# A graph layer on one core: eight groups of x rows, B's rows per group, and a later subtraction and store

## The chip, the core and the metric

The kernel runs on one core of a Trainium2 chip. The metric is the device time of one execution in microseconds (us). The kernel before was run three times: 1989.7, 1991.37 and 1993.4 us, median 1991.37. A further execution was profiled, and the profile's numbers all come from that one.

## What is computed

One layer of a graph network over 12500 nodes (64 features each) and 200000 edges (32 features each, sorted by destination), then a residual and a layer norm. All data are float32.

```python
msg_in = jnp.concatenate([nodes[row], nodes[col], edge_features], axis=-1)
messages = relu(msg_in @ mW1 + mb1) @ mW2 + mb2
aggregated = jax.ops.segment_sum(messages, col, num_segments=nodes.shape[0])
upd_in = jnp.concatenate([nodes, aggregated], axis=-1)
x = layernorm(x + relu(upd_in @ uW1 + ub1) @ uW2 + ub2)
```

`row` is the source node of an edge (`src`), `col` its destination (`dst`). Sources are spread at random over the nodes; destinations rise from edge to edge.

## The kernel before

**Tables.** The first product of a message has three terms: source row times a part of mW1, destination row times another part (plus mb1), edge features times the last part. The first two depend on a node alone, so the kernel computes them once per node: table A (`tab_a`, 12500 rows of 128 numbers) and table B (`tab_b`). A is made at the head in 13 chunks of eight blocks of 128 nodes (`chunk_a`): the queue of ACT loads columns of x (`xl`), PE multiplies them (L381), ACT copies one half of the result and DVE the other (L391, L389) into a tile `tb`, and ACT's queue stores it to A (L395). There are two buffers for `xl`, two for `tb`, two for the PSUM result. Only the first chunk of B is made at the head, into B and into a small copy `B0` that the early edges read; the other chunks of B follow among the edge steps (`chunk_b`, L397).

**Edges.** The edges lie in 1563 tiles of 128. Eight tiles are a group (`SUB`, 196 of them), sixteen a super (`SUP`, 98). For each tile:

- POOL gathers 128 source rows by an indirect DMA, one per tile (`gather`, L147, L158). For the first `XG` = 7 groups it takes the raw rows of x (256 B each), which are transposed and multiplied by PE in the loop (`transpose`, and L257 in `node_part`), since A doesn't exist yet. From group 7 on it takes rows of A (512 B), which DVE adds (L263). The rows go into a pool of six buffers (`ROWB`); two groups of x rows share one, a group of A rows fills one. `frees` says after which group's use a buffer can be taken again.
- SP loads 32 consecutive rows of B that start at the tile's first destination, a window, into a tile `rhs` (`windows`, L216). One call of `windows(g)` loads the 16 windows of super g. The starts are read from `wint`, or for the first 20 supers from `win0`, a copy cut off at B0's end (L433).
- PE multiplies, per tile, a stack of 32 edge features and 32 rows of selection by the stack of mW1's part and the window (`edge_part`, L243). The selection is built on DVE per super from destinations that SP has loaded (`loadd` L173, `select` L185), and SP loads the edge features behind it (`load`, L204).
- DVE adds the gathered row, ACT applies Relu (`node_part`, L263 and L264), PE multiplies the result by a second selection so that each tile gives sums over its 32 nodes (`collect`, L276), and DVE adds them into a table of sums `comb` in SBUF (`aggregate`, L288). The second selection compares `drc` with the slot numbers; `drc` is destination minus window start, made by the subtraction in `relative` (L351) from two SP loads, in three parts: 128 columns at the head, and two more in steps 1 and 2.

**Updates.** When a stretch of up to 384 nodes has all its edges, an update turns sums into output: `columns`, `update`, `residual`, `norm`, one step apart, 54 times. The last of them, `norm`, scales on DVE into a tile `o` and then stores it from SP (L335).

**Order.** Each engine and each queue works in the order in which the program issues, which is written out by hand: first the head (the loop over chunks at L435, which also clears `comb` in eight strips, L441, and loads x columns into it, L344), then one step per group at L537 to L573. A step s issues, among others, `norm` of an update, the windows of the next super (in even steps), `node_part(s)`, `collect` and `aggregate` of group s-1, `select` and `load` of the next super (even steps), `loadd` (odd steps), a chunk of B, and `edge_part(s+1)`. Group numbers and step numbers are the same. The second half of the program (L576 on) is a general path that is skipped for these inputs.

Of the kernel before, what the change touches and what calls it, by code (L numbers as in the profile page):

```python
# [34 lines left out]
PADWIN = 1000000  # L35
EK, SK = 0, DE
ROWB = 6
XG = 7
NCH = 8
HB = NCH // 2  # L40
EARLY = NCH * P
GE = 20
# [22 lines left out]
def gnn_kernel(ctx: ExitStack, tc: tile.TileContext, x1T, x, eT, e_rows, src, dst, dst_row, wrow, wnext, whalf,  # L65
# [22 lines left out]
    nc = tc.nc  # L88
# [4 lines left out]
    A = dram.tile([NPAD, DH], F32, name="tab_a")  # L93
# [50 lines left out]
    def tiles(s):  # L144
        return range(s * SUB, min((s + 1) * SUB, NT))

    def gather(s):  # L147

        if s >= XG or s % 2 == 0:
            buf = rows.tile([P, SUB, DH], F32, name="xg")  # L150
        else:
            buf = xg[s - 1][0]
        d = DH if s >= XG else D
        a = buf.rearrange("p k (b d) -> p (k b) d", d=d)
        if s < XG:
            a = a[:, s % 2 * SUB:(s % 2 + 1) * SUB, :]
        for i, t in enumerate(tiles(s)):
            nc.gpsimd.indirect_dma_start(  # L158
                out=a[:, i, :], out_offset=None, in_=A[:, :] if s >= XG else x[:, :],
                in_offset=bass.IndirectOffsetOnAxis(ap=src_s[:, t:t + 1], axis=0))  # L160
        xg[s] = buf, a

    with tc.tile_pool(name="sup", bufs=2) as sup, tc.tile_pool(name="work", bufs=2) as work, tc.manual_schedule():
# [39 lines left out]
                q = 64 * b + EK  # L203
                nc.sync.dma_start(L[g][q:q + DE], eT[g, b])  # L204

        def windows(g):

            nt = min(SUP, NT - g * SUP)
            r = rhs[g % 2]
            w, tab, n = (win0, B0, EARLY - WIN + 1) if g < GE else (wint, B, N)  # L210
            _, ws = nc.values_load_multi_w_load_instructions(
                w[0:1, g * SUP:g * SUP + nt], engines=[ET.SP], min_val=0, max_val=n - 1,
                skip_runtime_bounds_check_because="destinations are node numbers")
            for i in range(nt):
                q = SK + 64 * (i % 2)
                nc.sync.dma_start(r[q:q + WIN, i // 2, :], tab[bass.ds(ws[i], WIN), :])  # L216

        def transpose(s):

# [8 lines left out]
        def parts(n):  # L228

            if n == SUB:  # L230
                return [(slice(None), slice(None))]
            return [(slice(b, b + 1), slice((n - b + 1) // 2)) for b in range(2) if n > b]

        def edge_part(s):

# [11 lines left out]
        def node_part(s):  # L247

            n = len(tiles(s))
            pc = pcs.pop(s)  # L250
            h = work.tile([P, 2, SUB // 2, DH], F32, name="h")
            if s < XG:
                xt = xs.pop(s)
                for i in range(n):
                    k, b = divmod(i, 2)
                    q = 64 * b
                    nc.tensor.matmul(pc[:, b, k, :], xt[q:q + 64, k, :], w1a[q:q + 64], start=False,  # L257
                                     stop=i + 2 >= n)
                nc.scalar.activation(h, pc, AF.Relu)
            else:  # L260
                a = xg.pop(s)[1].rearrange("p (k b) f -> p b k f", b=2)
                for b, m in parts(n):
                    nc.vector.tensor_tensor(h[:, b, m], pc[:, b, m], a[:, b, m], op=ALU.add)  # L263
                    nc.scalar.activation(h[:, b, m], h[:, b, m], AF.Relu)  # L264
            hs[s] = h

        def collect(s):
# [57 lines left out]
            us[u] = (n0, py, mv, sd)  # L325

        def norm(u):
            n0, py, mv, sd = us.pop(u)
# [17 lines left out]
        def relative(a, b):  # L346

            wbc = work.tile([P, WCH], I32, name="wbc", tag="tb")
            nc.sync.dma_start(dst_s[:, a:b], dst[:, a:b])
            nc.sync.dma_start(wbc[:, :b - a], wrow[:, a:b].broadcast_to([P, b - a]))  # L350
            nc.vector.tensor_tensor(drc[:, a:b], dst_s[:, a:b], wbc[:, :b - a], op=ALU.subtract)  # L351
# [77 lines left out]
        for r in rhs:  # L429
            for o in (EK, EK + 64):  # L430
                nc.sync.dma_start(r[o:o + DE], mW1[2 * D:, :].unsqueeze(1).broadcast_to([DE, SUP // 2, DH]))
        relative(0, 8 * SUP)
        nc.vector.tensor_scalar(win0, wint[:, :GE * SUP], float(EARLY - WIN), None, op0=ALU.min)  # L433
        Q = NCOL // 4
        for k, c in enumerate(range(0, NB, NCH)):  # L435
            chunk_a(c)
            if k == 0:
                chunk_b(0, [B0v, Bv])
                windows(0)
            if k < 8:  # L440
                nc.vector.memset(comb[:P if k < 4 else ONE, k // 4, k % 4 * Q:(k % 4 + 1) * Q], 0.0)  # L441
# [95 lines left out]
        for s in range(last + 3):  # L537
            g, j = divmod(s, SUP // SUB)
            while gathered < NSUB and frees(gathered) < s:
                gather(gathered)  # L540
                gathered += 1
            if s - 2 in due:
                norm(due[s - 2])
            if j == 0 and g + 1 < NSUP:
                windows(g + 1)
            if s < NSUB:
                node_part(s)
            if s in due and s < last:
# [24 lines left out]
            rest(s)  # L573


    flag = nc.values_load(flag_i[0:1, 0:1], min_val=0, max_val=2 * EBULK,  # L576
# [163 lines left out]
```

## Time and profile before

| what | us |
|---|---|
| median of the three runs | 1991.37 |
| the profiled execution | 1995.25 |
| its span, first to last instruction | 1993.5 |
| PE busy, 7851 matmuls | 1364.8 (68%) |
| DVE busy | 908.7 (46%) |
| ACT busy | 348.4 (17%) |
| POOL busy, 1572 instructions | 1477.0 (74%) |
| DMA, mean over the span | 106 GB/s |
| TensorE clock granted, mean | 0.559 |

A profile row names a source line, an engine, an operation and the tiles it writes and reads; times are microseconds from the span's start. "Idle before" is the time for which the engine did nothing ahead of an instruction, and the name behind the arrow is what ended that wait, as far as semaphores tell. "issue" means that it waited for nothing that the profile shows. SPq and ACTq are the queues on which SP and ACT issue DMAs; the time in such a row is that of issuing, and the transfer lands later.

### The profile page before, as it was taken

What the parts mean: (1) busy time and instruction counts of PE and PEld (TensorE: products, weight loads), DVE (VectorE), ACT (ScalarE), POOL (GpSimd) and SP (SyncE); (2) the same over time, 40 slices, a digit from 0 to 9 for tenths busy, and PEclk for the clock granted to TensorE, in tenths of its full rate; (3) what the DMA queues carried; (4) which work ended last, traced back from release to release, by engine and by line L of the source; (5) the groups of instructions that cost most, each with busy time, mean ns of one, the idle gap of its engine ahead of it and who ended that gap; (6) DMA issues with size and microseconds to landing.
All of it is one profiled execution on the core that took longest, in us unless ns stands there. A gap on an engine that the chain in (4) does not pass through costs nothing.

```text
span 1993.5 us, 31593 instructions
## 1 busy us (share of the span) xinstructions
PE 1364.8 (68%) x7851; PEld 1211.9 (61%) x7851; DVE 908.7 (46%) x2661; ACT 348.4 (17%) x479; POOL 1477.0 (74%) x1572
## 2 busy tenths in 40 slices
PE   3678876656566666566667766676686776776867
PEld 3577875556555666556566665665575655665756
DVE  5347544434343444444444444444454545454544
ACT  1121111111111111111111111121212121212111
POOL 7577777777777777777777777777777777777773
PEclk7665555555555555555555555556555656565555
DMA  8745554433333333333333333334333333333331
GB/s 219 217 118 151 158 139 117 115 88 100 88 99 89 99 91 99 91 97 92 99 91 94 97 100 91 97 96 102 95 99 97 96 100 98 98 98 98 98 98 39
DMA packets 244401, 211.74 MB, mean 106 GB/s; under 512 B 80542, under 2 KB 209022, under 8 KB 243824
## 3 DMA queue, kind: packets, MB, share of 16 engines
q0 software_dynamic: 50016, 100.70, 20.4%
q1 hardware_dynamic: 178644, 98.69, 17.9%
q10 hardware_dynamic: 15554, 10.31, 1.8%
q8 instruction: 63, 1.03, 0.2%
q14 instruction: 124, 1.02, 0.2%
HBM read 190.78 MB, written 18.68 MB: 105 GB/s over the span
## 4 chain that ended last, share of the span: by engine, by line
POOL 53%; issue 25%; PE 9%; DMA 8%; DVE 3%; SPq 1%; ACT 1%; DVEq 0%; ACTq 0%; POOLq 0%
POOL xg L158 53%; DMA xg<-tab_a,src_s 5%; PE ph L276 3%; DMA xl<-in_x1T 2%; PE pc L243 2%; DVE comb L288 2%; PE pu L304 1%; PE py L315 1%; DVE h L263 1%; PE pb L381 1%; PE pu L305 1%; PE py L316 1%; DMA l<-in_eT 0%; PE ph L274 0%; DVE o L333 0%
## 5 line engine op out<-in xcount | busy, mean ns | idle before, releaser
L158 POOL DMA_INDIRECT xg<-tab_a,src_s x1507 | 1423.0, 944 | 470.0 <-issue 444.2
L276 PEld LDWEIGHTS ph<-sel,h 128*128 128x128 f32 x3126 | 610.2, 299 | 34.4 <-issue 34.4
L276 PE MATMUL ph<-sel,h 128*128 128x32 f32 x3126 | 601.0, 363 | 0.0
L263 DVE TENSOR_TENSOR h<-pc,xg 128x1024 f32<-128x1024 f32 (+1 forms) x190 | 230.8, 1215 | 770.4 <-DMA xg<-tab_a,src_s 720.7
L243 PE MATMUL pc<-rhs,l 64*128 64x128 f32 x3126 | 408.9, 415 | 62.8 <-DMA l<-in_eT 24.5
L288 DVE TENSOR_TENSOR comb<-comb,ph 128x64 f32 x1563 | 345.6, 221 | 202.1 <-ACT xw L297 83.0
L243 PEld LDWEIGHTS pc<-rhs,l 64*128 64x128 f32 x3126 | 352.7, 303 | 82.8 <-DVE rs L330 30.3
L264 ACT ACTIVATE h<-h 128x1024 f32<-128x1024 f32 (+1 forms) x190 | 199.2, 1049 | 915.0 <-DVE h L263 881.7
L304 PE MATMUL pu<-comb,w2u 128*128 x108 | 88.9, 927 | 255.9 <-DVE comb L288 255.9
L274 PE MATMUL ph<-selb,one 128*128 128x256 bf16 x196 | 75.4, 384 | 239.7 <-DVE comb L288 156.8
L274 PEld LDWEIGHTS <-one 128*128 128x128 bf16 x196 | 27.3, 139 | 272.2 <-DVE comb L288 252.8
L304 PEld LDWEIGHTS pu<-comb,w2u 128*128 128x128 f32 x108 | 27.1, 312 | 271.3 <-DVE comb L288 271.3
L185 DVE TENSOR_TENSOR l<-l,cps 128x1024 f32<-128x1024 int32 (+1 forms) x101 | 123.3, 1221 | 4.8 <-DMA l<-in_dst_row 1.3
L197 ACT CAST selb<-sel 128x512 bf16<-128x512 f32 x98 | 60.4, 616 | 329.3 <-DVE sel L189 308.7
L315 PE MATMUL py<-ux,xw 128*128 128x64 f32 x324 | 87.0, 362 | 0.7 <-ACT hTu L307 0.7
L316 PE MATMUL py<-u,hTu 128*128 128x64 f32 x324 | 84.3, 354 | 0.0
L305 PE MATMUL pu<-xw,uz 128*128 128x384 f32 x108 | 80.1, 846 | 0.0
L307 ACT ACTIVATE hTu<-pu,ub_s 128x384 f32<-128x384 f32 x54 | 31.3, 580 | 270.7 <-PE pu L305 270.7
L315 PEld LDWEIGHTS py<-ux,xw 128*128 128x128 f32 x324 | 68.9, 263 | 10.8 <-issue 6.3
L316 PEld LDWEIGHTS py<-u,hTu 128*128 128x128 f32 x324 | 70.3, 268 | 0.0
L189 DVE TENSOR_TENSOR sel<-cps,drc 128x512 f32<-128x512 f32 x98 | 66.8, 682 | 0.1
L158 POOL DMA_INDIRECT xg<-in_x,src_s x56 | 53.0, 946 | 18.4 <-issue 16.5
(73 smaller groups left out, 420.2 us busy)
## 6 DMA issues: line engine op xcount, KB each, us to landing
l<-in_dst_row SPq DMA_DIRECT2D x196, 128.0 KB
l<-in_eT SPq DMA_DIRECT2D x196, 128.0 KB
rhs<-tab_b SPq DMA_DIRECT2D x1563, 16.0 KB
xg<-tab_a,src_s POOLq DMA_INDIRECT x1507
tab_b<-tb SPq DMA_DIRECT2D x13, 512.0 KB
tab_a<-tb ACTq DMA_DIRECT2D x12, 512.0 KB
out<-o SPq DMA_DIRECT2D x54, 96.0 KB
comb<-in_x1T SPq DMA_DIRECT2D x6, 520.0 KB
```

What stands on the lines that cost most here:

```text
L158: nc.gpsimd.indirect_dma_start(out=a[:, i, :], out_offset=None, in_=A[:, :] if s >= XG else x[:, :], in_offset=bass.IndirectOffsetOnAxis(a ...
L185: nc.vector.tensor_tensor(l[r], l[r].bitcast(I32), node[r].unsqueeze(2).broadcast_to([r.stop - r.start, SUP // 2, P]), op=ALU.is_equal)
L243: nc.tensor.matmul(pc[:, b, k, :], L[g][q:q + 64, m, :], rhs[g % 2][q:q + 64, m, :], start=s >= XG or k == 0, stop=s >= XG)
L263: nc.vector.tensor_tensor(h[:, b, m], pc[:, b, m], a[:, b, m], op=ALU.add)
L264: nc.scalar.activation(h[:, b, m], h[:, b, m], AF.Relu)
L274: nc.tensor.matmul(ph[:, :n, 1, :], one0, SB[g][:, k0:k0 + n, :], start=True, stop=True)
L276: nc.tensor.matmul(ph[:, i, 0, :], h[:, i % 2, i // 2, :], S[g][:, k0 + i, :], start=True, stop=True)
L288: nc.vector.tensor_tensor(to, to, ph[:, i], op=ALU.add)
L304: nc.tensor.matmul(pu, w2u, comb[:, 0, bass.ds(n0, UB * P)], start=True, stop=False)
L305: nc.tensor.matmul(pu, uz, xw, start=False, stop=True)
L315: nc.tensor.matmul(py[:, i], xw[:, i * P:(i + 1) * P], ux, start=True, stop=False)
L316: nc.tensor.matmul(py[:, i], hT[:, i * P:(i + 1) * P], u2, start=False, stop=True)
```

## The change

Six edits go together.

- `XG` is 8: group 7 also takes rows of x and goes through transpose and matmul. The first gather from A is that of group 8, the 65th.
- `windows` takes a group in place of a super and loads its eight windows; step s issues `windows(s + 2)`, in each step. The head issues `windows(0)` and `windows(1)`.
- In the head, the subtraction of the first 128 columns (`relative`, with its two loads) moves from ahead of chunk one into chunk five (k == 4), and `win0` with the first windows from ahead of, and out of, chunk one into chunk three (k == 2).
- `norm` no longer stores; a new `store` issues the DMA at the end of the same step.
- A gathered group of A rows lies in its buffer in the order in which the PSUM tile holds it (even tiles, then odd ones), so the add reads and writes plain slices; `parts` returns slices for that.
- `columns` of the last update stands right behind `aggregate` in step 196.

```diff
-XG = 7
+XG = 8
...
-        d = DH if s >= XG else D
-        a = buf.rearrange("p k (b d) -> p (k b) d", d=d)
         if s < XG:
-            a = a[:, s % 2 * SUB:(s % 2 + 1) * SUB, :]
+            a = buf.rearrange("p k (b d) -> p (k b) d", d=D)[:, s % 2 * SUB:(s % 2 + 1) * SUB, :]
+        else:
+            a = buf.rearrange("p (b k) d -> p k b d", b=2)
...
-        def windows(g):
-            nt = min(SUP, NT - g * SUP)
+        def windows(s):
+            g = s // (SUP // SUB)
+            o = s % (SUP // SUB) * SUB
+            nt = len(tiles(s))
...
-                nc.sync.dma_start(r[q:q + WIN, i // 2, :], tab[bass.ds(ws[i], WIN), :])
+                nc.sync.dma_start(r[q:q + WIN, (o + i) // 2, :], tab[bass.ds(ws[i], WIN), :])
...
-                a = xg.pop(s)[1].rearrange("p (k b) f -> p b k f", b=2)
-                for b, m in parts(n):
-                    nc.vector.tensor_tensor(h[:, b, m], pc[:, b, m], a[:, b, m], op=ALU.add)
-                    nc.scalar.activation(h[:, b, m], h[:, b, m], AF.Relu)
+                hf, pf = (t.rearrange("p b k f -> p (b k) f") for t in (h, pc))
+                a = xg.pop(s)[0]
+                for m in parts(n):
+                    nc.vector.tensor_tensor(hf[:, m], pf[:, m], a[:, m], op=ALU.add)
+                    nc.scalar.activation(hf[:, m], hf[:, m], AF.Relu)
...
+            us[u] = (n0, o)
+
+        def store(u):
+            n0, o = us.pop(u)
             nc.sync.dma_start(out[bass.ds(n0, UB * P), :].rearrange("(c p) d -> p c d", p=P), o)
...
-        relative(0, 8 * SUP)
-        nc.vector.tensor_scalar(win0, wint[:, :GE * SUP], float(EARLY - WIN), None, op0=ALU.min)
...
             if k == 0:
                 chunk_b(0, [B0v, Bv])
+            if k == 2:
+                nc.vector.tensor_scalar(win0, wint[:, :GE * SUP], float(EARLY - WIN), None, op0=ALU.min)
                 windows(0)
+                windows(1)
+            if k == 4:
+                relative(0, 8 * SUP)
...
-            if j == 0 and g + 1 < NSUP:
-                windows(g + 1)
+            if s + 2 < NSUB:
+                windows(s + 2)
...
             if 1 <= s <= NSUB:
                 collect(s - 1)
                 aggregate(s - 1)
+            if s == NSUB:
+                columns(K - 1)
...
-            if s == NSUB:
-                columns(K - 1)
...
             rest(s)
+            if s - 2 in due:
+                store(due[s - 2])
```

More of the change, by code (lines that the diff above doesn't have):

```diff
@@ L152, in gather @@
             buf = xg[s - 1][0]
-        d = DH if s >= XG else D
-        a = buf.rearrange("p k (b d) -> p (k b) d", d=d)
         if s < XG:
-            a = a[:, s % 2 * SUB:(s % 2 + 1) * SUB, :]
+            a = buf.rearrange("p k (b d) -> p (k b) d", d=D)[:, s % 2 * SUB:(s % 2 + 1) * SUB, :]
+        else:
+            a = buf.rearrange("p (b k) d -> p k b d", b=2)
         for i, t in enumerate(tiles(s)):
             nc.gpsimd.indirect_dma_start(
-                out=a[:, i, :], out_offset=None, in_=A[:, :] if s >= XG else x[:, :],
+                out=a[:, i, :] if s < XG else a[:, i // 2, i % 2, :], out_offset=None, in_=A[:, :] if s >= XG else x[:, :],
                 in_offset=bass.IndirectOffsetOnAxis(ap=src_s[:, t:t + 1], axis=0))
@@ L211, in windows @@
             _, ws = nc.values_load_multi_w_load_instructions(
-                w[0:1, g * SUP:g * SUP + nt], engines=[ET.SP], min_val=0, max_val=n - 1,
+                w[0:1, s * SUB:s * SUB + nt], engines=[ET.SP], min_val=0, max_val=n - 1,
                 skip_runtime_bounds_check_because="destinations are node numbers")
@@ L230, in parts @@
             if n == SUB:
-                return [(slice(None), slice(None))]
-            return [(slice(b, b + 1), slice((n - b + 1) // 2)) for b in range(2) if n > b]
+                return [slice(0, SUB)]
+            return [slice(b * SUB // 2, b * SUB // 2 + (n - b + 1) // 2) for b in range(2) if n > b]
         def edge_part(s):
@@ L327, in norm @@
         def norm(u):
-            n0, py, mv, sd = us.pop(u)
+            n0, py, mv, sd = us[u]
             rs = work.tile([P, UB], F32, name="rs")
```

## The prediction

> **What bounds the kernel now.** I read the page's chain of work that ended last, then the waits of POOL, then POOL's timeline at both ends of its work, then DVE and SP between 0 and 80 us. The chain names the engine:
>
> ```profile
> POOL 53%; issue 25%; PE 9%; DMA 8%; DVE 3%; SPq 1%; ACT 1%; DVEq 0%; ACTq 0%; POOLq 0%
> ```
>
> POOL's gathers (L158) and the "issue" time between them make 78% of the span. POOL's waits (line, what it waited for: us in total, times, longest) and its timeline (start us, us, ..., idle before) show the one hole:
>
> ```profile
> POOL xg L158 <- issue: 460.7, 1511, 0.3
> POOL xg L158 <- DMA rhs<-tab_b: 10.9, 1, 10.9
> ```
>
> ```profile
> 72.20 0.94 POOL L158 DMA_INDIRECT xg<-in_x,src_s  x1 [0.30 <-issue]
> 84.04 0.94 POOL L158 DMA_INDIRECT xg<-tab_a,src_s  x1 [10.90 <-DMA rhs<-tab_b]
> ...
> 1965.22 0.95 POOL L158 DMA_INDIRECT xg<-tab_a,src_s  x1 [0.30 <-issue]
> ```
>
> A gather takes 0.944 us, the next starts 0.30 later: one per 1.249 us (the timeline's median). 1563 gathers, first at 2.88, last at 1965.22: 1562 x 1.249 = 1950.9 of 1962.3 us. Of the 11.4 left over, 10.6 is one wait, before the 57th gather, the first to read tab_a. The table is being written until then (its last store is issued at 78.93 on ACT), so I read the "rhs<-tab_b" in that row as a mislabel of tab_a's landing. After it POOL never waits again. Behind POOL the tail is 1993.5 - 1966.2 = 27.3 us. So the span is: start 2.9 + gathers at POOL's pace + 10.6 hole + 0.8 other + tail 27.3. PE, DVE and ACT follow the gathers (DVE's adds at L263 waited 720.7 us for them).
>
> **What the skill says.** "DMA: Bandwidth & Descriptors", section "SWDGE vs HWDGE vs iDMA": a GpSimd core runs code to compute the descriptors of a gather. The trace agrees: 128 rows cost 0.944 us of POOL from tab_a (512 B rows) and 0.946 from x (256 B rows), so the source of a group changes nothing in POOL's work. Same page, "Issuing engines are not separate DMA queues": transfers of SP, ACT and GpSimd run on the same 16 DMA engines. The trace agrees: the DMA share is 0.89 to 0.93 between 20 and 84 us, and ACT's loads of x columns slow down when SP's comb loads begin. Same page, "Anatomy of one DMA": the wait for a semaphore is on the issuing sequencer, so what is behind it on SP stands. The trace agrees: SP's waits hold 493 us before L204, for select. "SBUF — State Buffer", section "Who interferes with whom": a VectorE instruction with two SBUF inputs contends with a GpSimd instruction that reads SBUF. Two gathers agree: they took 1.71 and 1.26 us beside L351's subtractions (0.77 + 0.32 lost); L263, which has one input in PSUM, delays none.
>
> **The change, part by part.**
>
> *Eight groups of x rows.* Gathers 57 to 64 now read x and need no table. POOL goes on at 72.20 + 1.25 = 73.45 and fills the hole with 8 x 1.249 = 9.99 us of work; gather 65, now the first on tab_a, is ready to issue at 83.45. The number of gathers stays 1563. If tab_a is complete by 83.4, the hole is gone: -10.6. If the table lands as before (gather at 84.04), 0.6 is left: -10.0. The added work lies on PE and ACT: group 7 takes 4 transposes (1.1 us, L224), a copy (0.59, L225) and 16 matmuls (1.9 to 2.1, L257) in place of an add of 1.21 on DVE, about +2 to 3 us on the consumers' path, under POOL. The gathers of 73 to 83 us bring 8 x 128 x 256 B = 0.26 MB beside tab_a's last stores, about 1 us of DMA at the 240 GB/s of that stretch.
>
> *Subtraction in chunk five, win0 and the windows in chunk three.* Before, DVE stood 17.57 us at the head for the subtraction's operand:
>
> ```profile
> 19.68 0.29 DVE L351 TENSOR_TENSOR drc<-drc,wbc 128x128 f32<-128x128 int32 x1 [17.57 <-DMA wbc<-in_wrow]
> ...
> 20.29 0.67 DVE L389 COPY tb<-pb 128x512 f32<-128x512 f32 x1
> ...
> 22.71 2.75 DVE L441 MEMSET comb<- 128x3232 f32 x1 [0.62 <-issue]
> ```
>
> PE's products of chunk one are ready at about 12, so its copy can come 8 us earlier. From there a chunk costs DVE 0.62 (copy) + 0.62 (before the memset) + 2.75 = about 4 us: copies at 12.3, 19 (it waits for its tb buffer, the store of chunk one), 23.3, 27.8, 31.8. Before they were at 20.3, 25.4, 29.3, 33.2, 37.2: some 5 us gained at chunk five. Then it is partly given back: the subtraction now waits, in chunk five, for wbc, which SP issues behind win0 (about 24) and 16 window loads. These took 26.93 to 38.59 before, 0.5 to 0.73 each, so 8 to 11.7 us; with two issues more wbc goes out at 33 to 37 and lands 4.5 later (15.11 to 19.6 before): 37.5 to 41.5. DVE stands until then and clears one more strip of comb; the sixth copy comes at 41 to 44.5 (before: 41.06). SP's comb loads (before from 39.94 on, 3.4 MB) start at 35 to 39 and have the DMA engines nearly to themselves while DVE stands. What remains then is bound by bytes: before, 41 to 83.7. I estimate that tab_a is complete 7 us earlier to 3 us later than before, 77 to 87, most likely 80.5. That is ahead of 83.45, and the hole is closed. Cost taken: 0. A DVE subtraction beside a gather, by the 0.32 and 0.77 above for 411 and 1024 columns: up to 0.3 for 128 columns. Taken: 0.3.
>
> *Are the buffers free in time?* With the hole gone POOL reaches group g 10.6 us sooner, and its row buffer comes free only when the add of group g-6 is done. From L263's ends and the starts of the groups' first gathers before:
>
> ```profile
> 142.32 1.22 DVE L263 TENSOR_TENSOR h<-pc,xg 128x1024 f32<-128x1024 f32 x1 [1.71 <-PE pc L243]
> ...
> 173.80 1.23 DVE L263 TENSOR_TENSOR h<-pc,xg 128x1024 f32<-128x1024 f32 x1 [0.28 <-DMA xg<-tab_a,src_s]
> ```
>
> The add of group 8 ended at 143.5, that of group 11 at 175.0; POOL will want their buffers at 155.03 - 10.6 = 144.4 and 185.01 - 10.6 = 174.4. Had the consumers not moved, with the 2 us of added work they would be 1 to 3 us late. They begin when PE has done the last chunk, 78.25 before, and move forward with the table: at 3 us earlier the stall is nothing, at 0 it is about 2.6. After 250 us the lead is 45 us and more (278.56 to 324.88 for group 25). Taken: 0; kept for the range: up to 3.
>
> *Windows per group.* Same 1563 loads, 8 per step instead of 16 per two steps, each still two steps (20 us) ahead of its matmul. No load of B's rows is named among PE's waits before, so nothing is removed from the path. The windows of an odd group now stand on SP behind load (L204), which waits for select. Eight loads take 4.4 us (8.74 for 16 at 776.72), landing about 3: some 12 us of lead remain. Cost 0, under cover of the lead; if that is gone, PE and then POOL pay.
>
> *Store at the step's end.* SP waited 112.1 us in 52 times before L335 for DVE's o, with loads behind it, but no consumer was late for it. The store goes out a few us later; o has two buffers and 37 us between updates. 0. In the last step nothing stands behind it: 0 in the tail.
>
> *Gather layout and parts.* The add reads the same 1024 elements in another order; 1.215 us is bounded by 1.1 and 1.35 and lies under POOL. Last group: still two adds and two Relus. columns(K-1) moved within step 196, where no load, chunk or edge part is issued between the two places: 0.
>
> Sum: -10.6 + 0.3 = -10.3. The profiled execution took 1995.25, its span is 1993.5, with 1.75 around it; it becomes 1983.2 and 1984.95. It stood 3.9 above the median of the runs shown. On the median: 1991.4 - 10.3 = **1981.1**.
>
> **Rivals.** (1) The table is late: the deferred subtraction holds DVE, the last chunks slip, and the new first table gather finds a hole of 3 to 7 us (table at 86 to 90). For it: wbc behind 16 loads on SP, and one tb buffer given to wbc, so chunk six copies only when chunk five's store has landed. Against it: bytes, not DVE, bound 41 to 84 (DMA share 0.89 and more). Gives about 1986. (2) The consumers catch POOL at groups 14 to 17: 3 us, about 1984. (3) The hole closes but the end doesn't move: 1989 to 1991; against it, POOL works without a gap to 1965.22, and the tail hangs on its last groups. (4) Slower: SP's order. An odd group's windows wait behind load, hence for DVE's select; if SP fell behind by over its 12 us of lead, PE's edge part would start late in each of 98 supers, and POOL stop for buffers. Price: 1 us per super is 98 us. It decides once the 45 us of row-buffer lead are used too; to end 0.2% above the median the supers must lose 10.3 + 4 us beyond both leads. SP issues some 6 us in a 10 us step, which speaks against it. About 2010.
>
> **Numbers.** Forecast (1981.1, own range 1978 to 1984): 0.67. Rival 1: 0.15. Rival 2: 0.09. Rival 3: 0.05. Rival 4: 0.04. Within 0.2% (4 us, about what a measurement of this kernel can tell from no change) lies rival 3 alone: faster 0.91, same 0.05, slower 0.04. The range holds forecast and rivals 1 and 2 but for their tails: 1977.5 to 1987.
>
> **What would show it.** POOL without an idle time over 1 us between 2.9 and its last gather, which starts near 1954.9; 64 gathers from x; the subtraction (128 columns) between 37 and 42 with DVE idle before it; comb loads on SP from 35 to 39; steps from 72 to 77 on; a tail of 27 us. It is wrong if POOL shows a new wait near 83 us (rival 1) or for DVE between 120 and 185 (rival 2), if PE's edge parts wait for rhs (rival 4), or if POOL ends 10 us earlier and the span doesn't (rival 3).

## The result and the profile after

| | before | after |
|---|---|---|
| median of six runs, us | 1990.53 | 1997.91 |
| lowest and highest | 1988.38 to 1993.4 | 1994.82 to 2000.5 |
| the profiled execution | 1995.25 | 2000.5 |
| its span | 1993.5 | 1998.4 |
| end of POOL's last gather | 1966.17 | 1971.22 |
| from there to the end | 27.3 | 27.2 |

The ratio of after to before is 1.0034, 95% interval 1.0021 to 1.0047: the change made the kernel slower by about 7 us. It was predicted to be 10 us faster. The profiled spans differ by 4.9, and POOL's last gather ends 5.05 later, so what happened is to be read on POOL.

The chain that ended last, by engine, in the kernel after:

```profile
POOL 48%; issue 21%; DMA 15%; PE 11%; DVE 4%; ACT 1%; SPq 0%; DVEq 0%; ACTq 0%; POOLq 0%
```

POOL and its issue time are still the larger part, but DMA and PE have gained shares: the chain now leaves POOL in places. POOL's waits in the kernel after (line, what it waited for: us in total, times, longest) and its timeline (start, us, ..., idle before) say where:

```profile
POOL xg L158 <- issue: 440.4, 1444, 0.6
...
POOL xg L158 <- DVE h L266: 10.6, 2, 6.1
POOL xg L158 <- DMA rhs<-tab_b: 5.2, 1, 5.2
```

```profile
82.67 0.94 POOL L158 DMA_INDIRECT xg<-in_x,src_s  x1 [0.30 <-DMA tab_a<-tb]
88.83 0.94 POOL L158 DMA_INDIRECT xg<-tab_a,src_s  x1 [5.21 <-DMA rhs<-tab_b]
...
153.61 0.94 POOL L158 DMA_INDIRECT xg<-tab_a,src_s  x1 [4.58 <-DVE h L266]
...
189.63 0.94 POOL L158 DMA_INDIRECT xg<-tab_a,src_s  x1 [6.07 <-DVE h L266]
...
1970.27 0.94 POOL L158 DMA_INDIRECT xg<-tab_a,src_s  x1 [0.30 <-issue]
```

The one hole of 10.6 us has become three. Less the usual 0.30, they are 4.9 at the first gather from the table (now the 65th), 4.3 at the first gather of group 14 and 5.8 at that of group 17: 15.0 in place of 10.6. Smaller waits make 1.4 in place of 0.5. Together that is 5.3 more, which is the 5.05 but for 0.2. The gathers themselves go at 1.249 us as before.

**The first hole** comes from DVE. DVE's timeline in chunk five of the kernel after, and SP's ahead of it:

```profile
36.19 0.63 DVE L396 COPY tb<-pb 128x512 f32<-128x512 f32 x1
...
47.84 0.29 DVE L358 TENSOR_TENSOR drc<-drc,wbc 128x128 f32<-128x128 int32 x1 [11.03 <-DMA wbc<-in_wrow]
48.75 2.75 DVE L451 MEMSET comb<- 63x3232 f32 x1 [0.61 <-DVE drc L358]
51.42 0.62 DVE L396 COPY tb<-pb 128x512 f32<-128x512 f32 x1
```

```profile
29.05 12.03 SPq L218 DMA_DIRECT2D rhs<-tab_b  x16
41.12 0.42 SPq L356 DMA_DIRECT2D drc<-in_dst  x1
42.09 0.37 SPq L357 DMA_DIRECT2D wbc<-in_wrow  x1
42.51 0.88 SPq L204 DMA_DIRECT2D l<-in_eT  x2
43.43 27.11 SPq L351 DMA_DIRECT2D comb<-in_x1T  x7
```

The operand's load stands behind 16 window loads and leaves at 42.09; DVE waits 11.03 us for it and copies no chunk from 36.8 to 51.4. (The subtraction's operand also takes one of the two `tb` buffers, but the sixth copy follows the memset without an idle time, so no buffer held it.) The sixth chunk's copy is 10.4 us later than before (41.06), and the last store of the table is issued at 83.98 (before: 78.93). So 5 of the 10 us that the eighth group filled come back.

**The other two holes** come from the consumers, the engines that use the gathered rows and so free the row buffers. DVE's wait for the second part of the subtraction, before:

```profile
96.20 1.23 DVE L351 TENSOR_TENSOR drc<-drc,wbc 128x1024 f32<-128x1024 int32 x1 [5.68 <-DMA wbc<-in_wrow]
```

DVE in the kernel after, between 100 and 190 us:

```profile
101.90 1.22 DVE L358 TENSOR_TENSOR drc<-drc,wbc 128x1024 f32<-128x1024 int32 x1 [7.03 <-DMA rhs<-tab_b]
...
152.12 1.23 DVE L266 TENSOR_TENSOR h<-pc,xg 128x1024 f32<-128x1024 f32 x1 [0.28 <-issue]
...
182.01 1.76 DVE L505 TENSOR_REDUCE mm<-drc 128x1 f32<-128x1563 f32 x1
183.70 1.76 DVE L506 TENSOR_REDUCE mm<-drc 128x1 f32<-128x1562 f32 x1
...
188.13 1.23 DVE L266 TENSOR_TENSOR h<-pc,xg 128x1024 f32<-128x1024 f32 x1 [0.28 <-issue]
```

Group 8's add ends at 153.35 and group 14's first gather, which takes that buffer, starts at 153.61; group 11's add ends at 189.36 and group 17's gather starts at 189.63. Before, the adds ended at 143.5 and 175.0, and POOL came for the buffers at 155.03 and 185.01. The consumers are 10 and 14 us later than then; their lead of 10 to 11.5 us is used up. Ahead of these adds stand two things that the change did not touch: the second part of the subtraction (DVE waited 5.7 for its operand before, 7.03 now) and the work of step 10: small products of the update's weights and, with two reductions over `drc`, a check of the input (some 8 us on DVE in all).

### The profile page after: what moved, and what is told of

It reads as the page before. It is cut to its first block, busy times and chain, and to the rows that moved or that the text cites. A ratio compares the mean times of both kernels' runs of the same rounds, so it can differ in the third digit from the quotient of the medians.

```text
span 1998.4 us, 31764 instructions
## 1 busy us (share of the span) xinstructions
PE 1355.4 (68%) x7871; PEld 1202.9 (60%) x7871; DVE 907.4 (45%) x2660; ACT 348.7 (17%) x480; POOL 1477.0 (74%) x1572
## 3 DMA queue, kind: packets, MB, share of 16 engines
q14 instruction: 125, 1.02, 0.2%
## 4 chain that ended last, share of the span: by engine, by line
POOL 48%; issue 21%; DMA 15%; PE 11%; DVE 4%; ACT 1%; SPq 0%; DVEq 0%; ACTq 0%; POOLq 0%
POOL xg L158 48%; DMA xg<-tab_a,src_s 11%; PE ph L279 4%; PE pc L245 2%; DVE comb L291 2%; DMA tab_a<-tb 2%; PE pb L388 1%; PE pu L307 1%; PE pc L259 1%; PE py L318 1%; PE pu L308 1%; DVE h L266 1%; PE py L319 1%; PE ph L277 0%; DMA comb<-in_x1T 0%
## 5 line engine op out<-in xcount | busy, mean ns | idle before, releaser
L279 PEld LDWEIGHTS ph<-sel,h 128*128 128x128 f32 x3126 | 603.2, 295 | 33.9 <-issue 33.8
L279 PE MATMUL ph<-sel,h 128*128 128x32 f32 x3126 | 594.1, 360 | 0.0
L266 DVE TENSOR_TENSOR h<-pc,xg 128x1024 f32<-128x1024 f32 x189 | 229.5, 1215 | 769.2 <-DMA xg<-tab_a,src_s 735.1
L245 PEld LDWEIGHTS pc<-rhs,l 64*128 64x128 f32 x3126 | 351.5, 301 | 80.8 <-DVE rs L333 27.2
L267 ACT ACTIVATE h<-h 128x1024 f32<-128x1024 f32 x189 | 198.2, 1049 | 915.4 <-DVE h L266 823.8
L277 PEld LDWEIGHTS <-one 128*128 128x128 bf16 x196 | 27.1, 138 | 279.7 <-DVE comb L291 259.5
L307 PEld LDWEIGHTS pu<-comb,w2u 128*128 128x128 f32 x108 | 27.1, 311 | 265.2 <-DVE comb L291 265.2
L158 POOL DMA_INDIRECT xg<-in_x,src_s x64 | 60.6, 948 | 21.3 <-issue 18.3
```

What stands on the lines that cost most here:

```text
L158: nc.gpsimd.indirect_dma_start(out=a[:, i, :] if s < XG else a[:, i // 2, i % 2, :], out_offset=None, in_=A[:, :] if s >= XG else x[:, :], ...
L245: nc.tensor.matmul(pc[:, b, k, :], L[g][q:q + 64, m, :], rhs[g % 2][q:q + 64, m, :], start=s >= XG or k == 0, stop=s >= XG)
L266: nc.vector.tensor_tensor(hf[:, m], pf[:, m], a[:, m], op=ALU.add)
L267: nc.scalar.activation(hf[:, m], hf[:, m], AF.Relu)
L277: nc.tensor.matmul(ph[:, :n, 1, :], one0, SB[g][:, k0:k0 + n, :], start=True, stop=True)
L279: nc.tensor.matmul(ph[:, i, 0, :], h[:, i % 2, i // 2, :], S[g][:, k0 + i, :], start=True, stop=True)
```

## Experiments

The theory after the result: (a) the eighth group is right and closes the hole, if the table is in time; (b) the table is late since DVE waits in chunk five for a load that was queued last; (c) the holes at groups 14 and 17 are a consequence of POOL's earlier arrival, meeting old stalls of DVE (second subtraction, step 10) and the longer step of group 7. The rivals: the eighth group itself costs more than it gives (against a); the table is bound by bytes, and DVE's wait is covered (against b); the windows' or the store's new order delays the consumers (against c).

"Holes" below are the idle times of POOL less the usual 0.30, in the order: first gather from the table; group 13; group 14 (its first two gathers together); group 17. Each profile is of one execution. Medians stand beside those of the kernel before on the same chip; the ratio, with its 95% interval, rests on all the times and can differ a little from the ratio of the medians.

### First six runs: two chips on which POOL is not the bound

Four single edits were run together, two of them again on another chip. The first and its repeat, against the kernel before:

```diff
-XG = 7
+XG = 8
```

> The kernel before with one edit, eight groups of x rows. Theory (three stalls: the table is late because DVE waits for the deferred subtraction; group 7 as an x step holds the consumers; the checks on DVE in step 10 hold them again): the table is ready near 84 as before, the hole shrinks from 10.6 to about 0.6, but the eighth x step costs the consumers some 5 us, so POOL waits about 4 us before group 14 and 2 before group 17; POOL's excess over its pace is about 7 against 11.4, time about 1986.5 (4 below before). Rival (the new order of SP's queue makes the later stalls): no stall at groups 14 and 17 here, time about 1980.5.

> The kernel before with one edit, eight groups of x rows; a repeat on another chip, since on the first one the kernel before itself took 2808 us[...]. Theory (three stalls: the table is late because DVE waits for the deferred subtraction; group 7 as an x step holds the consumers; the checks on DVE in step 10 hold them again): the table is ready near 84 as before, the hole shrinks from 10.6 to about 0.6, but the eighth x step costs the consumers some 5 us, so POOL waits about 4 us before group 14 and 2 before group 17; POOL's excess over its pace is about 7 against 11.4, time about 1986.5 (4 below before). Rival (the new order of SP's queue makes the later stalls): no stall at groups 14 and 17 here, time about 1980.5.

The second and its repeat, against the kernel after: both loads of the first subtraction stay in the head, into a tile of their own, and only the subtraction is in chunk five.

```diff
+        w0 = first_loads(8 * SUP)
         Q = NCOL // 4
...
             if k == 4:
-                relative(0, 8 * SUP)
+                nc.vector.tensor_tensor(drc[:, :8 * SUP], dst_s[:, :8 * SUP], w0, op=ALU.subtract)
```

> The changed kernel, with the two loads of the deferred subtraction issued in the head ahead of the chunks, into a tile of their own; the subtraction stays in chunk five. Theory (DVE's wait for these loads delays the table): DVE doesn't wait in chunk five, the table is ready before 83.4, no hole before the 65th gather; consumers start at 78 or sooner; stalls at groups 14 and 17 stay in part (6 to 9 us in sum): 1986 to 1990. Rival (the table is bound by bytes, the comb loads beside it, whatever DVE does): hole of 2 to 5 us stays, time 1993 to 1998.

> The changed kernel, with the two loads of the deferred subtraction issued in the head ahead of the chunks, into a tile of their own; the subtraction stays in chunk five; a repeat on another chip. Theory (DVE's wait for these loads delays the table): DVE doesn't wait in chunk five, the table is ready before 83.4, no hole before the 65th gather; consumers start at 78 or sooner; stalls at groups 14 and 17 stay in part (6 to 9 us in sum): 1986 to 1990. Rival (the table is bound by bytes, the comb loads beside it, whatever DVE does): hole of 2 to 5 us stays, time 1993 to 1998.

The third, against the kernel after, moves the weights' products and the checks from step 10 to step 24; the fourth sets `XG` back to 7 in the kernel after.

```diff
-            elif s == BS + 2:
+            elif s == 24:
                 weights()
```

> The changed kernel with the products of the update's weights and the input checks in step 24 in place of step 10. Theory: the wait of 5.8 us before group 17 goes, the hole of 4.9 and the wait of 4.5 before group 14 stay: about 1992. Rival (the windows' order on SP makes the consumers late): the waits stay, 1998.

```diff
-XG = 8
+XG = 7
```

> The changed kernel with seven groups of x rows. Theory: the table is as late as in the changed kernel (gather at about 88.8), so the hole is about 15 us and no stall follows at groups 13 to 17; POOL's excess about 16, time 1995 to 1998, as the changed kernel. Rival (the eighth x group itself does the damage): back at 1990 to 1991.

On these two chips the kernel before itself took 2808.29 and 2807.17 us. In the first of these runs POOL was busy 53% of the span (74% in the profile before), DVE's adds into `comb` waited 907 us for something that the profile doesn't name, and 16 window loads in a row took SP up to 24.5 us, against 8.74 in the profile before. Why these chips are slower isn't shown. POOL was not the bound there, so the medians can't be read for these theories, and none of the expected times came. They were 2801.54 and 2807.89 (eight groups alone), 2821.83 and 2824.56 (early loads), 2823.61 (checks late) and 2829.03 (seven groups). The four kernels were then run once more, unchanged, on a chip where the kernel before took 1990.98.

### Eight groups alone

> The kernel before with one edit, eight groups of x rows[...]. Theory (three stalls: the table is late because DVE waits for the deferred subtraction; group 7 as an x step holds the consumers; the checks on DVE in step 10 hold them again): the table is ready near 84 as before, the hole shrinks from 10.6 to about 0.6, but the eighth x step costs the consumers some 5 us, so POOL waits about 4 us before group 14 and 2 before group 17; POOL's waits are about 7 in sum against 12 before, time 4 to 5 below before. Rival (the new order of SP's queue makes the later stalls): no stall at groups 14 and 17 here, time 10 below before.

Measured: 1988.88 against 1990.98, ratio 0.9976 (0.9962 to 0.9989). POOL's timeline:

```profile
82.91 0.94 POOL L158 DMA_INDIRECT xg<-tab_a,src_s  x1 [0.30 <-issue]
...
135.40 0.94 POOL L158 DMA_INDIRECT xg<-tab_a,src_s  x1 [2.65 <-PE pt L224]
...
149.54 0.95 POOL L158 DMA_INDIRECT xg<-tab_a,src_s  x1 [4.46 <-DVE h L263]
```

The hole is gone completely, as (a) says: the old head has the table ready at 83. But 6.8 of the 10.6 us come back at groups 13 and 14 (2.35, 4.15 and 0.26). The adds show why: group 6 is done 1.2 us later than before (133.8 against 132.6), group 8 5.8 later (149.3 against 143.5). From group 6 to group 8 the consumers lose some 4.5 us: group 7 now has its transposes and 16 matmuls. So the holes behind the table need neither the new windows nor the new store. They lie at groups 13 and 14, not at 14 and 17 as expected.

### Loads in the head, subtraction in chunk five

> The changed kernel, with the two loads of the deferred subtraction issued in the head ahead of the chunks, into a tile of their own. Theory (DVE's wait for these loads delays the table): no wait in chunk five, no hole before the 65th gather; a wait of about 4 before group 14 and of 5 before group 17 stay; POOL's waits 9 to 12 in sum, time 0 to 3 below before. Rival (the table is bound by bytes): a hole of 2 to 5 us before the 65th gather, time 3 to 7 above before.

Measured: 1993.09 against 1990.98, ratio 1.0011 (1.0003 to 1.0019); holes 0, 0.9, 4.5, 4.6. DVE, then POOL:

```profile
35.68 0.28 DVE L457 TENSOR_TENSOR drc<-drc,wbc 128x128 f32<-128x128 int32 x1
```

```profile
83.26 0.94 POOL L158 DMA_INDIRECT xg<-tab_a,src_s  x1 [0.30 <-issue]
```

DVE no longer waits, and the first hole of the kernel after (4.9) is gone: (b) is shown. The time is a miss all the same, 2.1 above where 0 to 3 below was expected: the holes behind stay. The rival has its part: chunks six to nine are copied up to 11 us earlier than before (chunk eight at 47.1 against 57.9), and yet DVE's last copy comes only 3.4 us earlier (73.9 against 77.3) and the last store of the table 0.9 (78.05 against 78.93); between 43 and 72 us, while SP's comb loads run, the DMA engines are busy 97% of the time. The early copies buy hardly any earlier table; a late copy makes it late.

### Checks late

> The changed kernel with the products of the update's weights and the input checks in step 24 in place of step 10. Theory: the wait of 5.8 us before group 17 goes, the hole of 4.9 and the wait of 4.5 before group 14 stay: 0 to 2 above before. Rival (the windows' order on SP makes the consumers late): the waits stay, 7 above before.

Measured: 1992.71 against 1990.98, ratio 1.0009 (1.0000 to 1.0019); holes 5.1, 1.1, 4.5, 0. The wait at group 17 (5.8) is gone and the others stay: the work of step 10 is its cause. What of it is the weights' products and what the checks, this edit doesn't tell apart.

### Seven groups in the kernel after

> The changed kernel with seven groups of x rows. Theory: the table is as late as in the changed kernel (first gather of it at about 88.8), so the hole is about 15 us and no stall of over 1 us follows at groups 13 to 17; POOL's waits 16 to 18 in sum, time 4 to 7 above before. Rival (the eighth x group itself does the damage): back at the time of before.

Measured: 1996.34 against 1990.98, ratio 1.0029 (1.0018 to 1.0040). POOL:

```profile
72.50 0.94 POOL L158 DMA_INDIRECT xg<-in_x,src_s  x1 [0.30 <-issue]
87.49 0.94 POOL L158 DMA_INDIRECT xg<-tab_a,src_s  x1 [14.05 <-DMA rhs<-tab_b]
```

All of the table's delay shows now: a hole of 13.7, and none after it. With eight groups the first hole was 8.8 smaller, and the holes at 14 and 17 took 10.0: with the late table and the unmended consumers the eighth group gives nothing in the sum.

### Loads early and checks late together

The early loads and step 10's work in step 24, on the kernel after.

> The changed kernel with both edits: the two loads of the deferred subtraction in the head, and the update's weights and the checks in step 24 in place of step 10. On a chip where the kernel before takes about 1990: theory (DVE's wait in chunk five delays the table by 5 us; the checks hold the consumers in step 10): no hole before the 65th gather, no wait before group 17, at most 4 us before group 14; 1980 to 1985, ahead of both kernels. Rival (table bound by bytes; SP's new order holds the consumers): 1993 to 1998. On a chip where the kernel before takes 2800, as in the first runs[...], neither theory's numbers can be read.

Measured: 1992.12 against 1993.64, ratio 0.9988 (0.9979 to 0.9998). The expectation was missed. Holes 0.1, 1.4, 4.5, 0: those of the table and of group 17 are gone, as in the single edits, but the one at group 14 stayed. My theory lacked a cause for it. What is left ahead of group 8's add is the second subtraction, which DVE meets in the step that has just issued its loads.

### The deferral alone

On the kernel before, with seven groups: the first subtraction goes to chunk five, `win0` and `windows(0)` to chunk three.

```diff
-        relative(0, 8 * SUP)
-        nc.vector.tensor_scalar(win0, wint[:, :GE * SUP], float(EARLY - WIN), None, op0=ALU.min)
...
+            if k == 2:
+                nc.vector.tensor_scalar(win0, wint[:, :GE * SUP], float(EARLY - WIN), None, op0=ALU.min)
                 windows(0)
+            if k == 4:
+                relative(0, 8 * SUP)
```

> The kernel before with the subtraction in chunk five and win0 with the first windows in chunk three, nothing else. Theory (DVE's wait in chunk five makes the table 4 to 5 us late, and with seven groups POOL is idle all that time): DVE waits 10 to 12 us in chunk five, the hole before the 57th gather is 13 to 15 us, no wait after it; 3 to 6 above before. Rival (another edit makes the table late): hole of 10 to 11, time of before.

Measured: 1997.51 against 1991.00, ratio 1.0037 (1.0024 to 1.0050). DVE, then POOL:

```profile
50.38 0.29 DVE L351 TENSOR_TENSOR drc<-drc,wbc 128x128 f32<-128x128 int32 x1 [13.27 <-DMA wbc<-in_wrow]
```

```profile
73.25 0.94 POOL L158 DMA_INDIRECT xg<-in_x,src_s  x1 [0.30 <-issue]
90.66 0.94 POOL L158 DMA_INDIRECT xg<-tab_a,src_s  x1 [16.46 <-DMA rhs<-tab_b]
```

This one part of the change costs 6.5 us alone, by the medians; 3 to 6 were expected. DVE's wait is 13.27, the hole 16.2, against 10.6 before.

### Windows by super again

The early loads, and both groups' windows in the even step, as in the kernel before.

```diff
-            if s + 2 < NSUB:
-                windows(s + 2)
+            if j == 0:
+                for t in (s + 2, s + 3):
+                    if t < NSUB:
+                        windows(t)
```

> The changed kernel with the early loads, and with the windows of both groups of a super issued in the even step, as before. Question: in the changed kernel with early loads POOL waited 4.6 us before group 17, in the kernel before with eight groups alone 0.3. If SP's new order (loadd behind eight window loads in the odd step, so that select in the even step waits for it) makes the difference, the wait before group 17 falls to 2 us or less here and the time is 2 to 4 below before; if not, it stays at 4 to 5 and the time within 2 of before. In both cases no hole before the 65th gather, and the wait of 4.3 before group 14 stays.

Measured: 1989.82 against 1991.00, ratio 0.9990 (0.9982 to 0.9998); holes 0.2, 2.5, 4.5, 0.5. Without the edit of the windows (early loads alone) they were 0, 0.9, 4.5, 4.6 and the ratio 1.0011. That looks like 4 us at group 17, but most of it is POOL's own place. The add of group 11, whose buffer group 17 takes, with early loads alone and then here:

```profile
182.14 1.22 DVE L266 TENSOR_TENSOR h<-pc,xg 128x1024 f32<-128x1024 f32 x1 [0.28 <-issue]
```

```profile
181.19 1.23 DVE L266 TENSOR_TENSOR h<-pc,xg 128x1024 f32<-128x1024 f32 x1 [0.28 <-DMA xg<-tab_a,src_s]
```

The consumers are only 0.9 us earlier. POOL itself comes to group 17 some 3 us later (182.2 against 179.1), since its first gather from the table was later (85.10 against 83.26) and it had lost 1.6 more at group 13. So the new order of the windows costs about 1 us at group 17. One way to it is in the trace: with it DVE waits 2.02 us at 170.82 for the operand of `select`, whose load stands behind eight windows on SP, and here it doesn't wait there. The time fell by 1.2 us (medians) or 2.0 (ratio), at or under the low end of the 2 to 4 expected. The two runs were on different chips, so the last few us between their ratios can't be put down to the windows.

The other side shows at group 2. Here `load` stands behind 16 windows and leaves at 90.45, and PE waits 3.86 us for `l`; with early loads alone it stands behind eight, leaves at 83.12, and PE doesn't wait. Group 2 is done at 98.7 here and at 89.8 there, of which 2.5 is the later start of group 0. At group 3 little is left of it (110.1 against 108.5): with eight windows DVE then waits 9.11 us for the second subtraction's operand, here 8.17.

### All three stalls mended

Early loads, checks late, and the second and third subtraction two steps behind their loads, on the kernel after. The two operands then hold both `tb` buffers for two steps, which no chunk needs in this stretch.

```diff
             if s == 1:
-                relative(8 * SUP, 8 * SUP + WCH)
+                sub_loads(8 * SUP, 8 * SUP + WCH)
             elif s == 2:
-                relative(8 * SUP + WCH, NT)
+                sub_loads(8 * SUP + WCH, NT)
                 halves(4 * SUP, NTP // 2)
+            elif s in (3, 4):
+                subtract()
```

> The changed kernel with early loads, with weights and checks in step 24, and with the second and third subtraction two steps behind their loads (steps 3 and 4 for 1 and 2). Theory (after the table the consumers are late by DVE's waits of 6 to 9 us for these loads, and that is what remains at groups 13 and 14): waits at groups 13, 14 and 17 together under 2 us, POOL's waits under 3 in sum against 12 before, 9 to 11 below before. If the wait before group 14 comes from the x step of group 7 alone: 4.3 stays, 5 to 7 below before.

Measured: 1982.69 (1981.34 to 1984.91) against 1991.00, ratio 0.9958 (0.9945 to 0.9971). That is 8.3 below before, a little less than the 9 to 11 expected; set against the same kernel before, the kernel after had 1.0034. POOL's timeline:

```profile
84.04 0.94 POOL L158 DMA_INDIRECT xg<-tab_a,src_s  x1 [1.41 <-DMA rhs<-tab_b]
...
143.98 0.94 POOL L158 DMA_INDIRECT xg<-tab_a,src_s  x1 [0.33 <-DVE h L266]
...
1954.53 0.94 POOL L158 DMA_INDIRECT xg<-tab_a,src_s  x1 [0.30 <-issue]
```

1.1 is left of the first hole, and nothing at groups 13, 14 and 17. Group 14's row says 0.33 behind the add of group 8: that add (137.4 to 143.7 are the ends of groups 7 and 8) has just come in time. From the run with loads early and checks late, this kernel differs in the two later subtractions alone, and the wait of 4.5 at group 14 is gone (0.3 is left at its second gather). The last gather starts at 1954.53.

### The mended consumers without the rest of the change

The kernel before with `XG` = 8, the two later subtractions split as above and the checks in step 24; first subtraction, windows and store as before.

> The kernel before with eight groups, weights and checks in step 24, and the second and third subtraction two steps behind their loads; order of SP, windows and store as before. Theory: hole of 0 to 0.6 before the 65th gather, waits at groups 13 and 14 under 2 us together; 8 to 11 below before, about as the changed kernel with all three mended. If the deferral, once its loads are early, gives the table a lead that counts, this one is 2 to 4 slower than that.

Measured: 1988.27 against 1991.00, ratio 0.9984 (0.9974 to 0.9993); holes 0.2, 0.6, 4.4, 0. Expected were 8 to 11 below before and under 2 us at groups 13 and 14: missed. The wait at 14 is there again, though DVE no longer waits for the second subtraction. Adds and Relus of the groups show that the consumers start later: group 2 is done at 95.2, in the run before this one at 91.5. PE's edge part of group 2, in this kernel and then in the one with all three mended:

```profile
90.14 2.27 PE L243 MATMUL pc<-rhs,l 64*128 64x128 f32 x15 [3.49 <-DMA l<-in_eT]
```

```profile
88.35 1.16 PE L245 MATMUL pc<-rhs,l 64*128 64x128 f32 x16
```

PE waits 3.49 us for `l`, whose loads stand on SP behind windows: 16 in this kernel, issued from 78.90 on for 7.85 us, so that `load` leaves at 86.79; eight in the other, so that it leaves at 84.49 and PE doesn't wait. Here windows per group gain. Group 8's add ends 4.7 us later than in the other kernel (148.4 against 143.7); how much of that is this wait, and whether another part of the change has a share in it, no run separates.

This points to two stalls in a row ahead of group 14: PE's for `l` behind 16 windows, and DVE's for the second subtraction. With neither mended (eight groups alone) the hole was 4.4, with the windows alone (loads early and checks late) 4.5, with the subtractions alone (this run) 4.4, and with both 0.3. Mending one of them shows nothing while the other stands. (These runs differ in the head and in step 10 too.)

### Mended consumers with seven groups

The kernel with all three mended, and `XG` = 7.

> The changed kernel with all three mended, but with seven groups of x rows. It shows what the eighth group is worth once nothing else holds POOL. Theory (the table is ready at about 84, POOL is free for it at 73.4): hole of 10 to 12 before the 57th gather, no wait after it, POOL's waits 11 to 13 in sum; time within 2 of before, 8 to 11 above the same kernel with eight groups. Rival (the mended consumers, not the eighth group, made that kernel faster): 3 to 8 below before.

Measured: 1997.05 against 1994.39, ratio 1.0009 (1.0000 to 1.0017). POOL:

```profile
73.35 0.95 POOL L158 DMA_INDIRECT xg<-in_x,src_s  x1 [0.30 <-issue]
84.26 0.95 POOL L158 DMA_INDIRECT xg<-tab_a,src_s  x1 [9.96 <-DMA rhs<-tab_b]
```

The hole is back at 9.7 and nothing follows it. The mending alone gives nothing; the eighth group takes 8.6 off the hole once the consumers can follow. (The medians by their ratios are 10 us apart. This profile also has a wait of 1.5 among the gathers from x, two gathers stretched by 1.3 in sum, and the slower of two paces, see the end; what share these have in the medians isn't known.)

## Why the prediction was wrong

**The bound, the mechanism of the hole, the tail: right.** POOL's last gather sets the end (27.2 behind it, as before; in the experiments behind the first six runs 23.3 to 27.3, so the span doesn't follow it to the us), and eight groups fill the hole: with the old head it vanished whole (eight groups alone), and with a mended one to 1.1. The last gather in the mended kernel starts at 1954.53, where the prediction wanted it (1954.9). That it agrees to 0.4 is in part luck: 1.4 of waits are left, and the 1.08 that subtractions had cost gathers before is gone. The source of a row doesn't change POOL's pace: right.

**"Most likely 80.5. That is ahead of 83.45, and the hole is closed. Cost taken: 0": failed.** The table came 5 us after the old time, since two terms were mis-sized. `wbc` went out at 42.09, not at 33 to 37. `win0` came at 27.70 (24 taken): the third chunk's copy was at 27.1, not at 23.3 (ACT, which copies first, had stood 8.10 us for a store of a table). Then 16 windows and their two neighbours on SP took 13 us, beyond the row of 8 to 11.7 that I had. The load needed 5.8 more (4.5 taken), so the subtraction was at 47.84, not 37.5 to 41.5, and the sixth copy at 51.4, not 41 to 44.5. "Bytes, not DVE, bound 41 to 84" was half true: bytes refuse an early table, as the early loads show, but that needs DVE's copies to keep the bytes coming. From 40 to 60 us, before and after (us, engines' busy time, clock, and last the DMA share and GB/s):

```profile
40.00:60.00 20.00, 7.78 (x48) 6.37 (x48) 9.19 (x7) 1.36 (x3) 14.63 (x17) 0.50 0.93 246
```

```profile
40.00:60.00 20.00, 3.21 (x26) 2.63 (x22) 9.64 (x6) 1.17 (x2) 14.34 (x16) 0.50 0.88 186
```

The share of busy DMA time, on which the prediction rested, hardly fell, but 60 GB/s less over 20 us is 1.2 MB, some 5 us at 246 GB/s (an estimate). That is the delay of the table. The comb loads did have the DMA engines "nearly to themselves", and so the engines moved less: 171 GB/s between 43 and 51 us. I had bounded this as rival 1 and put 0.15 on it; its 3 to 7 us is what came (4.9).

**"Are the buffers free in time? Taken: 0": failed, and by more.** With the eighth group the consumers lost 4.5 between groups 6 and 8, not 2 to 3; "they move forward with the table" became a later start; and the row of DVE that I used, the add of group 8 at 143.5, stood behind a wait of 5.7 for the second subtraction that I did not look for. In the old kernel such waits lay under the hole of 10.6 and cost nothing. To close the hole was to take their cover away: what I had asked of the first subtraction (whose operand is late?) was to be asked of the second and of the checks in step 10 as well. Rival 2 named groups 14 to 17 with 3 us; it came with 10.0.

**The rivals were weighed as if they excluded each other.** Rivals 1 and 2 have one cause between them: a late table starts the consumers late. Together they made 15.0 of holes in place of 10.6, and no case of mine held a time above the old one but the order on SP.

**Windows: "cost 0", wrong both ways by a few us.** About 1 us lost at group 17 against the order by super, and PE's wait for `l` at group 2 gone, which was 2.4 to 4.1 in the four experiments with 16 windows in a row; that paid only once the second subtraction was mended. The prediction looked among PE's waits for B's rows and found none; what stood behind their issues was `load`. Rival 4's mechanism (a queue on SP behind windows) is there, but at two places, not in each of 98 supers. Store, row layout and the moved `columns`: the mended kernel has all three and lies near its predicted time, so that nothing of size can be in them unless two effects cancel; none was run alone. The 0.3 for the subtraction beside a gather was 0.07 in the kernel after (one gather of 1.02 at 47.93). Gathers stretched by the later parts cost 0.44 (before: 1.08).

## What to carry to other kernels

Before a stall of the bounding engine is filled, list every wait of its followers within the next buffers' depth: they were free under the stall, and become the new bound as soon as it is gone. A moved computation takes its loads with it; leave the loads where the queue is empty and move only the use. A high share of busy DMA time doesn't say that bytes flow: read the GB/s beside it. Where two stalls stand in a row, a test that mends one shows nothing. And where two rivals share a cause, work out the case in which both happen.

## What the hardware showed beyond that

The gathers go at one of two paces, and a whole execution keeps to one: their mean duration was 0.9434 to 0.9448 us in most profiles, and 0.9457 to 0.9469 in five, with a start every 1.248 to 1.249 or 1.251 us. The same kernel showed both (eight groups alone, and the early loads, each in the first run and its repeat), and so did each of the two chips, so it is neither the program nor the chip; what it is, no run shows. Over 1563 gathers 0.0024 us make 3.7 us, about the 4 us that the prediction took as the least change to be told; single profiles of 1990 us should not be compared without the pace beside them.

A VectorE subtraction with both inputs in SBUF stretched some of the gathers beside it, from 0.944 us to at most 1.87. The Trainium skill's "SBUF — State Buffer", section "Who interferes with whom", which says that a VectorE instruction with two SBUF inputs contends with a GpSimd instruction that reads SBUF, is borne out, and the traces show what sets the price: which of the two began first. A gather that began before the subtraction kept its 0.94 (the run with all three mended: gather at 106.51, subtraction 106.63 to 107.84). A gather that began during it lost the time from its start to the subtraction's end, less 0.12 to 0.13:

| run | gather starts | subtraction ends | left | lost |
|---|---|---|---|---|
| before | 96.53 | 97.42 | 0.90 | 0.77 |
| before | 107.28 | 107.72 | 0.44 | 0.31 |
| after | 102.57 | 103.13 | 0.56 | 0.44 |
| eight groups alone | 95.39 | 95.70 | 0.31 | 0.19 |
| eight and mended | 110.57 | 111.62 | 1.05 | 0.93 |
| all three mended | 107.76 | 107.84 | 0.08 | 0.00 |

In the profiles of all runs 21 gathers began during such a subtraction, and 20 of them fit this. The other (windows by super, at 35.68) began in the same hundredth of a microsecond as the subtraction and kept its 0.94. So the price of one subtraction was between nothing and 0.93 us, by chance of when it fell.
